# Attention scores in groups of three, maxima by head over all keys, and the maxima's split on GpSimd

## The chip, the cores and the metric

The kernel runs on one core of one Trainium2 chip. The metric is the device time of one execution in microseconds (us). The core has five engines with a queue each, and an engine works through its queue in order: PE (TensorE, matrix products; PEld is its loading of weights), DVE (VectorE), ACT (ScalarE), POOL (GpSimd) and SP (SyncE, which issues DMAs here). [...]

## The reference

Two sandwiched layers on x of 8 batches x 1024 tokens x 256 features: attention with 16 query heads of 16 features and 4 key/value heads, then a linear layer with ternary weights. All in float32.

```python
# x: (8, 1024, 256); H = 16, Hkv = 4, hd = 16
def attn(x):
    q = rope(x @ Wq); k = rope(x @ Wk); v = x @ Wv      # k, v: 4 heads, each used by 4 query heads
    scores = einsum('bhqd,bhkd->bhqk', q, k) / sqrt(256)
    o = einsum('bhqk,bhkd->bhqd', softmax(scores), v)
    return o.reshape(B, S, D) @ Wo

def ffn(x):
    delta = 0.7 * mean(abs(weight))
    w = where(weight > delta, 1, where(weight < -delta, -1, 0)) * alpha
    return einsum('bsd,od->bso', x, w) + bias

x = x + layernorm(attn(layernorm(x)))
x = x + layernorm(ffn(layernorm(x)))
```

## The kernel before

**Units, blocks, steps.** The work goes in 16 units of 512 query tokens, half a batch each. A unit has four blocks (the four query heads j of each of the four key/value heads r, so a block holds four heads x 512 queries), and a block has eight steps, one for each 128 keys: 512 steps in all. `NSTEP`, `SPU` = 32 steps in a unit, `NK` = 8 steps in a block, `UQ` = 512.

**Scores twice.** The scores are computed in two layouts. For the maximum of each query (line 569, tiles `sm`) queries are the weights of the product and 512 keys stream through, so that queries lie on the partitions; DVE then takes the maximum over the keys (line 577, into `mx`). For the exponentials (line 624, tiles `se`) 128 keys are the weights and 512 queries stream, so that keys lie on the partitions; ACT takes exp into `e` (line 632), and `e` is the streaming operand of the product with v (line 645, tile `av`). The maximum of each query is subtracted inside the second product: it rides in two more rows of the queries' operand `q_st`. These rows are made from `mx` by `shift_split` (lines 585 to 590, three small DVE operations: the larger of the two key halves, its high part, its low part), then by `shift_rows`: a transpose on PE (`pm`, line 596), a copy by ACT (`mh`, line 598) and two DMAs from SP's queue (line 605).

**Halves of the array.** Each of these score products has a contraction over 64 rows, so it takes one half `a` (0 or 1) of PE's rows, and two products on different halves can run at once. The product with v has 128 rows and 32 columns: four of them, one for each r, take the four column groups. It is in plain float32 and PE runs it as two passes, so that the profile counts two matmuls for each of the program's.

**The order.** PE, DVE and ACT get their instructions in the order in which the program writes them; POOL gets an order from the planner of the framework, but for the start and the end of the kernel, where its order is written out as well. `step(n)` (line 997) writes one step: `exp_half(n, r2)` and `max_half(k, r2)` are generators that give one score product each, interleaved as se, sm, se, sm, four of each in a step. The sm belong to a step that is `LEAD` = 11 steps ahead. A maximum tile has two banks, which hold the two halves `a` for the same 512 keys: its two products are on different halves of the array, and the reduce gives two values per query. After the scores come the parts of other work that are due in this step (`todo`), and last `av_step(n - 1)`, the four products of the step before with v over 512 queries, 128 keys.

**Other work.** `P_PARTS` and `T_PARTS` (lines 896 to 912) give the step at which each part of the projections of a later unit (`Project`) and of the tail of an earlier unit (`Tail`: output projection, layer norms, ternary layer) is written. Their products go through one bank of the pool of `se`, and are called `pq`, `pkv`, `pa`, `pf` (256 columns each, 12, 12, 12 and 8 of them in a part), `pt_xt`, `pt_ot` (four transposes in a part) and `ptv`. POOL does their elementwise work (layer norm applied, rotation of q, splits in high and low parts).

**Buffers.** In PSUM: two maximum tiles of two banks (`ps_mx`), three banks for `se` and all other products (`ps_e`), one for `av` (`ps_av`). `e` tiles: four buffers of 128 x 2 x 512.

**Ends.** In the last 11 steps the maxima are done; then `se` goes to the maximum tiles' banks, two halves in one, and one ACT instruction takes the exponential of 1024 columns (line 635).

Of the kernel before, what the change touches and what calls it, by code (L numbers as in the profile page):

```python
# [17 lines left out]
H = 16  # query heads  # L18
HKV = 4  # key/value heads, r below; query head = 4 * r + j
G = H // HKV  # L20
HD = 16
UT = 4  # token tiles in a unit
UQ = UT * P  # tokens in a unit
# [5 lines left out]
def kernel(  # L29
# [18 lines left out]
    """Two sandwiched layers: x += LN(attn(LN(x))), x += LN(ffn(LN(x))).  # L48

    The work goes in units of 512 query tokens.  Scores are computed twice: with queries on the  # L50
    partitions for each row's maximum, and with keys on the partitions for exp and the product
    with V.  For the scores q and k are split into high + low parts of 12 significant bits, which
    single-pass float32r products carry exactly: the contraction runs over
    [q_hi, q_hi, q_lo] against [k_hi, k_lo, k_hi].  The maximum, split alike, rides into the second
    pass as two more rows of the contraction, against rows of -1 in the keys.  V carries columns
    of ones, which give the softmax's denominators.  Heads r = 2 * r2 + a take the row half a of
    TensorE in the scores, and its column group r in the product with V.
    """
# [10 lines left out]
    SPU = G * NK  # steps in a unit  # L69
    NSTEP = NU * SPU  # L70
    LEAD, START = 11, 10  # steps by which the maxima run ahead, and do so at the start
# [6 lines left out]
    ep = ctx.enter_context(tc.tile_pool(name="ep", bufs=4))  # L78
# [17 lines left out]
    # ---- constants and weights  # L96
# [35 lines left out]
    # Operands with parts that never change: rows of -1 in k, of 0 in q, columns of ones in v.  # L132
# [7 lines left out]
    def fill_rows(st, value, lo, n):  # L140
        """Rows lo .. lo + n of each half."""
        flat = "p c t -> p (c t)" if len(st.shape) == 3 else "p j c t -> p (j c t)"
        for a in range(2):
            dst = st[64 * a + lo : 64 * a + lo + n].bitcast(F32).rearrange(flat)
            width = dst.shape[1]
            nc.sync.dma_start(
                out=dst, in_=fill_d[value : value + 1, 0:width].to_broadcast([n, width])
            )
# [15 lines left out]
    def split(eng, hi, lo, src, hi_eng=None):  # L164
        """src in two parts of 12 significant bits."""
        split_hi(hi_eng or eng, hi, src)
        split_lo(eng, lo, src, hi)

    # Weights in parts.  The columns of w_q go by their place in a pair.
# [9 lines left out]
    # A bank of PSUM for all that is not scores or their product with v.  Before and after those,  # L179
    # the banks of the maxima serve as well.  # L180
# [9 lines left out]
    # Ternary weights, transposed: wt[d, o] = (w[o, d] > delta) - (w[o, d] < -delta)  # L190
# [4 lines left out]
    def measure():  # L195
        ffn["ones"] = work.tile([P, P], F32, tag="qt", name="ones")
# [33 lines left out]
    # ---- layernorm over the last axis of [P, 2, D]  # L230
    def ln_stats(src):
        """(mean, -mean, 1 / sqrt(var + eps)) of each tile."""
# [29 lines left out]
    def transposed(src, tag, name, copy=nc.scalar.copy):  # L262
        """[P, 2, D] -> [P, ND, 2 * P], features on the partitions."""
# [6 lines left out]
        dst = work.tile([P, ND, 2 * P], F32R, tag=tag, name=name)  # L270
# [3 lines left out]
    TERMS = ((0, 0), (0, 1), (1, 0))  # parts of the operands in a product  # L274
# [4 lines left out]
    def product(out, left, right, terms=TERMS):  # L279
        """The sum of left[i][:, c]^T right[j][:, c]."""  # L280
# [13 lines left out]
    def rotate(eng, x, cos, sin, t2):  # L294
        """x of [P, 2, n], the two of a pair on the same partition, in place."""
# [5 lines left out]
    # ---- projections of a unit: q and k rotated, transposed and split, v.  q comes out transposed,  # L301
    # with the two columns of a pair on the same partition.
    dq = {}

    class Project:
        """Its parts, each with at most one use of PSUM.  k's pairs are rotated with tokens on the
        partitions in the first units, and in the others by a way over DRAM."""

        def __init__(self, u, eng):
# [4 lines left out]
            if u not in (1, 2):  # L314
# [3 lines left out]
                self.xs = [xs[:, :, 2 * p : 2 * p + 2, :] for p in range(2)]  # L318
            else:  # the unit before still holds those
# [4 lines left out]
                    ep.tile([P, 2, 2, D], F32R, tag="e", name=f"xs_{u}_{p}") for p in range(2)  # L324
# [9 lines left out]
        def hi(self, p, eng=None):  # L334
            split_hi(eng or self.eng, self.xs[p][:, 0], self.xn[p])

        def lo(self, p, eng=None):
            split_lo(eng or self.eng, self.xs[p][:, 1], self.xn[p], self.xs[p][:, 0])
# [7 lines left out]
        def x(self, p, l):  # L346
            self.xt[p, l] = transposed(self.xs[p][:, l], f"xt{l}", f"xt{l}_{self.u}_{p}")

        def kv(self, p):
            """k and v, transposed."""  # L350
# [8 lines left out]
        def v(self):  # L359
            """v, and k where it doesn't go over DRAM, with tokens on the partitions."""  # L360
# [33 lines left out]
        def k(self):  # L394
            """Its parts, transposed, one on each half of the partitions."""
# [7 lines left out]
            self.hl["k"] = qkp.tile([P, UQ], F32R, tag="hlk", name=f"hlk_{self.u}", bufs=2)  # L403
            nc.scalar.copy(self.hl["k"], pt.bitcast(F32))

        def kv_and_dram(self):
            """And k to [(token tile, pair), place, token]."""
# [10 lines left out]
        def kt(self):  # L418
# [3 lines left out]
            )  # fmt: skip  # L422
# [20 lines left out]
        def rotate_q(self, p, eng=None):  # L443
# [3 lines left out]
            t2 = work.tile([P, 2, 2 * P], F32, tag="t2", name=f"t2_{self.u}_{p}")  # L447
# [25 lines left out]
        def stack_keys(self):  # L473
            """[hi, hi, lo] of k in each row half."""
# [9 lines left out]
    def row_pickers():  # L484
        """Matrices that pick the rows of the stacks of q and of k, and k's rows of -1."""
# [22 lines left out]
    class PickRows:  # L508
        """Stacks of the first units, by products with those matrices."""
# [26 lines left out]
    def stack_queries(u):  # L536
        """[hi, lo, hi] of q in each row half."""
# [9 lines left out]
    # ---- each query's largest score, of the four heads of a block (unit, j)  # L547
    mx = {}

    def block_queries(i, r2=slice(None)):  # L550
        """The queries of a block in their stack: of head j, or in the last unit of a token tile."""
# [5 lines left out]
    def max_half(k, r2):  # L557
        i, m = divmod(k, NK)
        u = i // G
        ch, t = divmod(m, UT)  # L560
        queries = block_queries(i, r2)
        queries = queries[:, t * P : (t + 1) * P] if u < NU - 1 else queries[:, t]
        ks = k_st[(u // UPB) % 3]
        if m == 0 and r2 == 0:
            mx[i] = small.tile([P, 2, UT, 2, 2], F32, tag="mx", name=f"mx_{i}")
        sc = ps_mx.tile([P, 2, 512], F32, tag="sm", name=f"sm_{i}_{m}_{r2}")
        for a in (1, 0):
            rows = slice(64 * a, 64 * a + 64)
            nc.tensor.matmul(  # L569
                sc[:, a, :],  # L570
                queries[rows],
                ks[rows, r2, ch * 512 : (ch + 1) * 512],
                start=True,
                stop=True,
            )
            yield
        nc.vector.tensor_reduce(mx[i][:, ch, t, :, r2], sc, AX.X, ALU.max)  # L577

    mhl = {}

    def shift_split(i):
        """The maxima of a block, split."""
        m = mx.pop(i)
        mc = small.tile([P, UT, 2, 2], F32, tag="mc", name=f"mc_{i}")
        nc.vector.tensor_tensor(mc, m[:, 0], m[:, 1], ALU.max)
        hl = mhl[i] = small.tile([P, 2, 2, 2 * UT], F32R, tag="mhl", name=f"mhl_{i}")
        order = "(r t)" if i // G < NU - 1 else "(t r)"
        hi, lo = (hl[:, :, l].rearrange(f"p a {order} -> p t a r", r=2) for l in range(2))
# [567 lines left out]
```

## Time and profile before

| | |
|---|---|
| median of 3 runs | 1691.28 us (1685.82 to 1694.91) |
| profiled execution, its span | 1693.0 us |
| granted PE clock in the profiled execution, mean | 0.988 of full |
| maxima: DVE reduces, line 577 | 1024 x 1.217 us mean |
| exponentials: ACT, line 632 | 2004 x 0.605 us mean |
| score products on PE, lines 624 and 569 | 2048 each, 64x512 |
| products with v on PE, line 645 | 4096 passes of 128x512, 0.606 us mean, overlapped |
| POOL busy | 834.1 us (49% of the span) |

A profile row gives a line of the kernel, engine, operation, the output and input tiles, the shapes, the count, then the busy time and the mean length of one; after the second bar stands the idle time of the engine just before these instructions and what ended most of it. Matmuls overlap in PE, and their ends are modelled, so starts of PE's instructions tell more than lengths. A timeline row gives the start, the length, and what was run; neighbours of one kind are merged.

### The profile page before, as it was taken

Reading aid. Unit: us, or ns where it says so; the run is one execution under the profiler, and the core shown is the slowest. Engines: PE = TensorE matmul, PEld = TensorE weight load, DVE = VectorE, ACT = ScalarE, POOL = GpSimd, SP = SyncE. Lnnn points to the kernel's source line nnn. Section 1 sums busy time; section 2 is a strip of 40 time slices with the busy share of each in tenths; the row PEclk is TensorE's granted clock in tenths of the full one; section 3 lists DMA queues with packets and bytes.
Section 4 is the critical chain, followed back from the end, with each engine's and each line's share of the span. In section 5 each row is a group of like instructions: output and inputs, shape, how many; then the busy total and the mean of one; then the engine's idle time right before and its main releaser. Section 6 shows DMA issues by size and latency. Waiting matters only on the chain.

```text
span 1693.0 us, 27812 instructions
## 1 busy us (share of the span) xinstructions
PE 1572.8 (93%) x10200; PEld 712.9 (42%) x10200; DVE 1404.3 (83%) x1815; ACT 1254.2 (74%) x2457; POOL 834.1 (49%) x1239
## 2 busy tenths in 40 slices
PE   7989989999999999999999999999999999999998
PEld 5534343443434444443443434444443443333344
DVE  7877778888898888978888898888888888888884
ACT  4667767777777777777777777777777777777775
POOL 5543364473734637454473735637464362333354
PEclk8999999999999999999999999999999999999999
DMA  4341424134251412514133251412414132141100
GB/s 135 71 90 30 97 68 101 46 79 85 65 96 52 85 58 79 98 48 97 58 73 79 72 101 44 92 53 72 86 53 92 46 79 61 32 85 33 41 14 26
DMA packets 86040, 117.38 MB, mean 69 GB/s; under 512 B 12088, under 2 KB 50808, under 8 KB 85752
## 3 DMA queue, kind: packets, MB, share of 16 engines
q1 hardware_dynamic: 85904, 115.60, 29.7%
q8 instruction: 81, 1.33, 0.3%
q14 instruction: 55, 0.45, 0.1%
HBM read 68.65 MB, written 45.88 MB: 68 GB/s over the span
## 4 chain that ended last, share of the span: by engine, by line
PE 52%; DVE 18%; POOL 10%; ACT 10%; issue 6%; DMA 3%; SPq 1%; POOLq 0%; DVEq 0%; ACTq 0%
PE av L645 19%; PE se L624 17%; DVE mx L577 13%; ACT e L632 9%; PE sm L569 3%; PE pa L283 3%; PE pf L283 2%; PE pq L283 2%; PE pt_xt L267 2%; POOL hl L162 1%; PE pt_ot L267 1%; PE pkv L283 1%; DVE bnst L237 1%; DVE mhl L589 1%; POOL t L297 1%
## 5 line engine op out<-in xcount | busy, mean ns | idle before, releaser
L577 DVE TENSOR_REDUCE mx<-sm 128x2 f32<-128x1024 f32 x1024 | 1199.6, 1217 | 246.2 <-PE se L624 176.4
L632 ACT ACTIVATE e<-se 128x512 f32<-128x512 f32 x2004 | 1045.7, 605 | 315.0 <-PE sm L569 286.8
L624 PE MATMUL se<-q_st,k_st 64*128 64x512 f32 x2048 | 739.4, 445 | 77.7 <-ACT e L632 53.6
L569 PE MATMUL sm<-k_st,q_st 64*128 64x512 f32 x2048 | 758.3, 460 | 12.0 <-DVE mx L577 10.8
L624 PEld LDWEIGHTS se<-q_st,k_st 64*128 64x128 f32 x2048 | 338.5, 185 | 699.1 <-ACT e L632 432.6
L645 PE MATMUL av<-e,v_aug 128*32 128x512 f32 x4096 | 548.1, 606 | 0.0
L569 PEld LDWEIGHTS sm<-k_st,q_st 64*128 64x128 f32 x2048 | 327.2, 185 | 59.1 <-DVE mx L577 42.5
L241 POOL TENSOR_SCALAR lnsc<-mv 128x2 f32<-128x2 f32 (+1 forms) x134 | 26.1, 194 | 432.6 <-DVE mv L239 427.6
L645 PEld LDWEIGHTS av<-e,v_aug 128*32 128x32 f32 x4096 | 80.8, 108 | 87.7 <-issue 53.6
L780 POOL TENSOR_TENSOR a<-a,bias_bc 128x512 f32<-128x512 f32 x30 | 38.4, 1280 | 144.7 <-ACT a L779 144.7
L719 POOL TENSOR_TENSOR xn<-xn,a 128x512 f32<-128x512 f32 x30 | 38.4, 1280 | 122.7 <-DMA a<-d_rec 114.4
L242 POOL TENSOR_TENSOR lnsc<-lnsc,mhalf 128x2 f32<-128x2 f32 (+1 forms) x134 | 92.2, 688 | 0.9
L162 POOL TENSOR_TENSOR hl<-xn,hl 128x512 fp32r<-128x512 f32 x60 | 76.4, 1284 | 0.5
L253 POOL TENSOR_SCALAR xn<-x,lnsc 128x256 f32<-128x256 f32 x116 | 64.8, 566 | 3.5
L283 PE MATMUL pa<-woh,hl 128*128 128x256 f32 x240 | 47.3, 296 | 2.6 <-POOL hl L162 1.2
L237 DVE BATCH_NORM_STATS2 bnst<-a 128x6 f32<-128x256 f32 x120 | 44.5, 413 | 4.1 <-POOL a L780 4.1
L297 POOL TENSOR_TENSOR t<-q_rot,sin_q_sb 128x512 f32<-128x512 f32 x31 | 39.7, 1280 | 14.5 <-ACT q_rot L438 14.3
L283 PE MATMUL pq<-xt,wqkvh 128*128 128x256 f32 x256 | 45.9, 303 | 0.2 <-ACT e L632 0.2
L237 DVE BATCH_NORM_STATS2 bnst<-x 128x6 f32<-128x256 f32 x124 | 46.0, 413 | 0.2 <-DMA x<-in_L_attn_x 0.2
L271 ACT CAST xt<-pt_xt 128x512 fp32r<-128x512 f32 x64 | 39.1, 617 | 4.4 <-PE pt_xt L267 4.4
L271 ACT CAST ot<-pt_ot 128x512 fp32r<-128x512 f32 x66 | 40.7, 618 | 1.9 <-PE pt_ot L267 1.9
L162 POOL TENSOR_TENSOR hlq<-q_rot,hlq 128x512 fp32r<-128x512 f32 x31 | 39.7, 1282 | 4.7 <-ACT hlq L159 4.5
(155 smaller groups left out, 1273.9 us busy)
## 6 DMA issues: line engine op xcount, KB each, us to landing
q_st<-dq SPq DMA_DIRECT2D x90, 256.0 KB
dq<-hlq SPq DMA_DIRECT2D x60, 256.0 KB
d_av<-avsb SPq DMA_DIRECT2D x60, 256.0 KB
x<-in_L_attn_x SPq DMA_DIRECT2D x15, 512.0 KB
xn<-d_av SPq DMA_DIRECT2D x30, 256.0 KB
a<-d_rec SPq DMA_DIRECT2D x30, 256.0 KB
xr<-in_L_attn_x SPq DMA_DIRECT2D x15, 512.0 KB
out_x<-a SPq DMA_DIRECT2D x30, 256.0 KB
```

The source lines that it names most:

```text
L162: eng.tensor_tensor(lo, src, hi.bitcast(F32), ALU.subtract)
L237: nc.vector.bn_stats(st[:, t, :], src[:, t, :])
L242: nc.gpsimd.tensor_tensor(sc[:, 1, :], sc[:, 1, :], mhalf[:, :n], ALU.pow)
L253: eng.tensor_scalar(dst[:, t, :], src[:, t, :], sc[:, 0, t : t + 1] if eng is nc.gpsimd else mv[:, t, 0:1], sc[:, 1, t : t + 1], ALU.add i ...
L271: copy(dst, pt.bitcast(F32))
L283: nc.tensor.matmul(out, chunk(left[i], c), chunk(right[j], c), start=(k == 0), stop=(k == len(steps) - 1),)
L297: eng.tensor_tensor(dst, x, table.unsqueeze(1).to_broadcast(list(x.shape)), ALU.mult)
L569: nc.tensor.matmul(sc[:, a, :], queries[rows], ks[rows, r2, ch * 512 : (ch + 1) * 512], start=True, stop=True,)
L577: nc.vector.tensor_reduce(mx[i][:, ch, t, :, r2], sc, AX.X, ALU.max)
L624: nc.tensor.matmul(sc if len(queries.shape) == 2 else sc.rearrange("p (j t) -> p j t", j=G), ks[rows, r2, kt * P : (kt + 1) * P], queries[ ...
L632: nc.scalar.activation(e[:, a, :], sc, AF.Exp, scale=1.0 / D**0.5)
L645: nc.tensor.matmul(av_ps[0][32 * r : 32 * r + 32, :], va[:, kt, r, :], e[r // 2][:, r % 2, :], start=(kt == 0), stop=(kt == NK - 1),)
```

## The change

The order of the work is written by groups instead of steps. A *quarter* is one score product of the exponential kind, four to a step; a block has 32 quarters.

- A group ("window") has three quarters: three se and three sm, alternating, then the parts of other work of any step that ended in this group, then the product with v for the group that lies two groups back. Of a block's 32 quarters, ten groups take three and the last two. One group at the start has two so that the maxima's order comes out; the last 11 steps go in groups of four.
- The product with v of a group takes as many columns as the group has quarters, times 128: the columns of all eight steps of a block are counted through, 4096 in all, and a group of three takes 384 of them. Where these cross from one step's 512 to the next's, two pieces are issued, each for all four r (`av_piece`). It accumulates into the same `av` bank.
- A maximum tile has the same size as before, but holds both halves of the keys for one `a`, that is one head: its two sm are on the same half of the array, and the reduce gives one value per query. (In the first block the order before is kept.) The larger of two key halves is no longer taken by an operation of its own.
- The split of the maxima in a high and a low part goes from DVE to POOL.
- `e` tiles hold 512 columns; there are 12 of them. The half `a` changes every two quarters instead of every quarter. Some small buffers become single or move, to make room.
- In the last 11 steps each 512 columns of exponentials are an ACT instruction of their own.

The comments and docstrings of the kernel are gone in the changed version, which does nothing to the program.

```diff
-    ep = ctx.enter_context(tc.tile_pool(name="ep", bufs=4))
+    ep = ctx.enter_context(tc.tile_pool(name="ep", bufs=12))
...
-    def max_half(k, r2):
...
+    def max_scores(v):
+        i, k = divmod(v // 2, 2 * NK)
+        u, part = i // G, v % 2
+        if i == 0:
+            a, ch, t, r2 = 1 - part, k // NK, k // 2 % UT, k % 2
+        else:
+            a, ch, t, r2 = 1 - k % 2, part, k // 4, k // 2 % 2
...
+        nc.tensor.matmul(
+            sm[0][:, part, :],
+            queries[rows],
+            k_st[(u // UPB) % 3][rows, r2, ch * 512 : (ch + 1) * 512],
...
+        else:
+            nc.vector.tensor_reduce(mx[i][:, a, t, r2 : r2 + 1], sm[0], AX.XY, ALU.max)
+        if k == 2 * NK - 1:
+            shift_split(i)
+            due.append((v // 4 + (1 if i < 2 else 2), i))
...
     def shift_split(i):
         m = mx.pop(i)
-        mc = small.tile([P, UT, 2, 2], F32, tag="mc", name=f"mc_{i}")
-        nc.vector.tensor_tensor(mc, m[:, 0], m[:, 1], ALU.max)
...
-        nc.vector.tensor_copy(hi, mc)
-        nc.vector.tensor_tensor(lo, mc, hi.bitcast(F32), ALU.subtract)
+        split(nc.gpsimd, hi, lo, m)
...
+    def exp_one(s):
+        n, (a, r2) = s // 4, divmod(s % 4, 2)
+        i, kt = divmod(n, NK)
+        e = es[n, r2, a] = ep.tile([P, UQ], F32, tag="e", name=f"e_{i}_{kt}_{r2}_{a}")
+        sc = ps_e.tile([P, 512], F32, tag="se", name=f"se_{i}_{kt}_{r2}_{a}")
+        exp_scores(n, r2, a, sc)
+        nc.scalar.activation(e, sc, AF.Exp, scale=1.0 / D**0.5)
...
+    def av_piece(i, first, end):
...
+        for kt in range(first // UQ, (end - 1) // UQ + 1):
+            lo, hi = max(first - kt * UQ, 0), min(end - kt * UQ, UQ)
+            for r in (1, 2, 3, 0):
+                nc.tensor.matmul(
+                    av_ps[0][32 * r : 32 * r + 32, lo:hi],
+                    va[:, kt, r, :],
+                    es[i * NK + kt, r // 2, r % 2][:, lo:hi],
+                    start=(kt == 0 and lo == 0),
+                    stop=(kt == NK - 1 and hi == UQ),
+                )
...
+    def maxima_by(s):
+        return s + 4 * START + 2 * (s >= 28) + 2 * (s >= 36)
...
+    def parts_of_step(n):
+        if due and due[0][0] <= maxima_by(4 * n + 4) // 4 - 1:
+            shift_rows(due.pop(0)[1])
+        for f, args in todo.pop(n, ()):
+            f(*args)
...
+    def window(i, s, size, late):
+        if done:
+            av_out(done.pop())
+        if late:
+            for r2 in range(2):
+                exp_two(s // 4, r2)
+        else:
+            end = min(maxima_by(s + size), 4 * NSTEP)
+            for q in range(max(size, end - maxima[0])):
+                if q < size:
+                    exp_one(s + q)
+                if maxima[0] < end:
+                    max_scores(maxima[0])
+                    maxima[0] += 1
+        behind.append((i, s, size))
+        for n in range(s // 4, (s + size) // 4):
+            parts_of_step(n)
+        av_windows(1 if late else 2)
```

## The prediction

> **What bounds the kernel now.** I read the page's busy shares and costliest groups first, then single steps on the timelines of PE, DVE and ACT, then the interval between units.
>
> ```profile
> span 1693.0 us, 27812 instructions
> ...
> PE 1572.8 (93%) x10200; PEld 712.9 (42%) x10200; DVE 1404.3 (83%) x1815; ACT 1254.2 (74%) x2457; POOL 834.1 (49%) x1239
> ...
> L577 DVE TENSOR_REDUCE mx<-sm 128x2 f32<-128x1024 f32 x1024 | 1199.6, 1217 | 246.2 <-PE se L624 176.4
> L632 ACT ACTIVATE e<-se 128x512 f32<-128x512 f32 x2004 | 1045.7, 605 | 315.0 <-PE sm L569 286.8
> ```
>
> PE is never long idle, and DVE's and ACT's idle time ends with scores from PE. But 93% is not 93% of work; one step shows that. Columns: start, length, instructions.
>
> ```profile
> 811.63 0.50 PE L624 MATMUL se<-q_st,k_st 64*128 64x512 f32 x1
> ...
> 812.81 0.50 PE L624 MATMUL se<-q_st,k_st 64*128 64x512 f32 x1
> ...
> 813.25 1.07 PE L645 MATMUL av<-e,v_aug 128*32 128x512 f32 x8
> 814.24 0.49 PE L624 MATMUL se<-q_st,k_st 64*128 64x512 f32 x1
> ...
> 814.58 0.62 PE L624 MATMUL se<-q_st,k_st 64*128 64x512 f32 x2
> 814.85 0.49 PE L569 MATMUL sm<-k_st,q_st 64*128 64x512 f32 x1
> 815.42 0.49 PE L624 MATMUL se<-q_st,k_st 64*128 64x512 f32 x1
> ...
> 816.00 0.50 PE L267 MATMUL pt_xt<-ident_r,xs 128*128 128x128 f32 x4
> 816.43 1.06 PE L645 MATMUL av<-e,v_aug 128*32 128x512 f32 x8
> ```
>
> ```profile
> 812.44 2.35 DVE L577 TENSOR_REDUCE mx<-sm 128x2 f32<-128x1024 f32 x2 [0.30 <-PE se L624]
> 815.04 2.36 DVE L577 TENSOR_REDUCE mx<-sm 128x2 f32<-128x1024 f32 x2 [0.25 <-PE se L624]
> ```
>
> ```profile
> 814.77 2.06 ACT L632 ACTIVATE e<-se 128x512 f32<-128x512 f32 x4 [0.55 <-PE sm L569]
> ```
>
> I call one se and the sm issued with it a pair. A step without other work lasts 814.24 - 811.63 = 2.61 us: pairs at 0, 0.34, 0.6 and 1.18, the v product 0.44 after the last (812.81 to 813.25), and 0.99 more to the next step. The fourth pair comes late because there are three banks for se: ACT starts 0.53 after the first se, takes 0.60, and the bank is free at 815.37. That wait (0.35 us) is what groups of three remove. DVE's reduce starts 0.46 after a tile's second sm; two follow 1.14 apart (2.35 - 1.21), so DVE waits only 0.25 to 0.30 of 2.61.
>
> ```profile
> L706 DVE RECIPROCAL den<-den x10: 540/542/544, 402.3 to 1312.3; 128x64 f32<-128x64 f32 x10
> ```
>
> This runs once a unit, so a unit takes 910.0 / 9 = 101.1 us. Its 32 steps clean are 83.5; 17.6 come from the other work. From last-pair-to-v-product intervals less 0.44, that is on PE: five of 12 matmuls (pq, pa, pkv) 1.67 each, two pf 1.19, eight groups of transposes 0.57 (815.42 to 816.43), ptv 0.43, four pm 0.21: 16.6. The last 1.0 is DVE and ACT.
>
> **The change, part by part.**
>
> *Groups of three.* A block (32 quarters; eight steps before) becomes ten groups of three pairs and one of two. An unblocked group has pairs at 0, 0.34, 0.6, then 0.35 to 0.44, then the v product. The two rounds of that start about 0.46 apart (1.07 less the row's mean of 0.605); a quarter fewer columns takes 0.115 off each: 0.99 - 0.23 = 0.76, bounds 0.74 (all scales) and 0.99 (nothing does). I take 0.77. That makes 1.75 a group, 3.5 for six quarters against 3.92 now: a gain, if nothing else waited.
>
> *The tiles that straddle.* Something else does. Three pairs are one and a half maximum tiles, and there are still two tiles. Call the tiles of two groups A, B, C: B gets its first half in the third pair of one group and its second in the first pair of the next, after the v product. From that pair: 0.56 to B's reduce (0.46, and the first matmul after a v product lasts 0.50 where later ones last 0.39), 1.14 to C's, 1.21 for it, 0.05 to the sm that was waiting for C's buffer (a reduce that ended at 804.66 released the one at 804.71). That sm is the next B's first half, in a third pair; behind it in PE's queue are the v product and the next group. So 0.44 + 0.77 more, and the cycle closes: 0.56 + 1.14 + 1.21 + 0.05 + 0.44 + 0.77 = 4.17 us for six quarters, 0.25 more than now, with PE standing 0.6 in every second group. A block: 5 x 4.17, and the short group 0.34 + 0.44 + 0.77 = 1.55, less some 0.4 that its whole tile and its 256 columns give back: 22.0 against 20.9. A unit: +4.5. The three se banks no longer bind: a bank is free 1.18 after its se and is wanted after 1.75.
>
> *What hides in the wait.* Groups of odd place (they end with C whole) have 0.6 us of room; in the others each microsecond goes straight into the cycle. By the due steps, modulo 8, parts at 0, 2, 3, 5, 6 fall into odd groups: six transposes (3.4), ptv (0.4), one pq and one pf (0.6 each can hide): 5.0 a unit. All of it stood on the path before. Ends: nothing, and 20 x 0.6 = 12.
>
> *Split v products.* Every fourth 512 columns end inside a group, so five of the eleven are issued as 128 and 256 columns: two more rounds of four matmuls. Nothing in the trace is so narrow in column groups; a round's four weight loads (0.108 us each, partly together) may outlast 128 columns. From 0.05 for both rounds to 0.7 (each as long as a full one); nearest are the transposes of 128 columns, four in 0.34 (0.50 less 0.16), little over their streaming, so 0.15. Three a block lie where nothing hides them: 3 x 4 x 0.15 = +1.8.
>
> [...]
>
> *Split of the maxima to GpSimd.* DVE loses L585, L589 and L590, about 0.62 a block; DVE has spare time except in the 2.35 of B and C, so a quarter counts: -0.6 a unit (0 to -2.5). POOL is in order. In the block whose maxima end while q is rotated it is full:
>
> ```profile
> 850.45 1.28 POOL L297 TENSOR_TENSOR q_rot<-q_rot,cos_q_sb 128x512 f32<-128x512 f32 x1
> 851.70 0.70 POOL L242 TENSOR_TENSOR lnsc<-lnsc,mhalf 128x2 f32<-128x2 f32 x1
> 852.37 0.72 POOL L298 TENSOR_TENSOR q_rot<-q_rot,t 128x256 f32<-128x256 f32 x1
> 853.06 0.72 POOL L299 TENSOR_TENSOR q_rot<-q_rot,t 128x256 f32<-128x256 f32 x1
> 853.78 1.08 POOL L253 TENSOR_SCALAR xn<-x,lnsc 128x256 f32<-128x256 f32 x2
> ```
>
> In the changed order the high part stands before L298 and the low part after L253: done near 855.4 with two small operations of 0.2 to 0.35 each, where PE's transpose pm ran at 853.15. PE is in order, so the v product and all scores stand behind it. The distance from pq to pm grows from 8.3 to about 8.8 us, so 1.7 of wait, 0.6 of it in an odd group's room: +1.0 a unit (0 to 2.4). In the other three blocks POOL is idle before pm or has 3 us to spare: nothing.
>
> *pm to the first se of its block.* The two DMAs of the maxima were issued 1.06 to 2.4 us after pm (802.35, 803.40, 1.35 for both) and had landed by 806.37, where the se ran without a wait: 2.4 to 4.0 after pm. Now only two v products and the short group lie between, 2.6. Up to 1.4, I take 0.7; three of a unit's four short groups carry a pq, pa or pf that covers it: +0.7 a unit (0 to 5.6). SP issues the same DMAs in the same order.
>
> The rest is worth nothing: the twelve smaller e tiles are released two groups ahead of use; the last eleven steps give ACT four exps of 0.49 instead of two of 1.03.
>
> Sum: 4.5 - 5.0 + 1.8 - 0.6 + 1.0 + 0.7 = +2.4 us a unit; over 15 units (the pipeline's start and the late steps left out, taken as unchanged within 5) +36 on the span of 1693.0, 1729. The median of the runs is 1.7 below that execution: 1727.
>
> **Rivals.** *The removed wait wins (faster).* For it: 0.35 us of waiting leave each step, PE and DVE shares are 93% and 83%, and PE with no wait would need 4 x (10 x 1.75 + 1.55 + 0.75) + 16.6 = 96 a unit. It needs more than 7.4 us of the other work under DVE's wait instead of 5.0, for instance because parts in even groups delay the reduces less than PE. At 97.5 a unit: 1693 - 54 - 2 = 1637. Against: the cycle through B and C holds whatever PE does. *Nothing hides:* parts and statistics on DVE fall between B and C, so that the 5.0 is lost: +7.4, 1802. *Narrow rounds cost full:* 0.7 instead of 0.15: +6.6 a unit more, 1826. *GpSimd late in every block:* 1.7 in four blocks: +5.8 more, 1814; POOL's idle time before pm in three blocks speaks against it.
>
> **How the numbers follow.** Forecast (slower by 0.5 to 4.5%) 0.42; nothing hides, narrow rounds or a late GpSimd 0.23 together; the wait's removal wins 0.27; cases that cancel within 0.5%, about what three runs (0.27% around their median) can tell, 0.08. Slower 0.65, same 0.08, faster 0.27. The likeliest's own range is 1700 to 1770; the range takes in half of each side: 1637, the faster rival's price, and 1814, that of the late GpSimd.
>
> **What would show it.** The changed trace should have pairs of groups near 1.7 and 2.5 us, with third pairs released by DVE mx; L632's waits on PE fewer and no se waiting for ACT e; a unit near 103.5; one pm a unit waiting for POOL. Wrong it is if groups of 1.7 follow each other without that wait, if reduces stand end to end, or if v products of two pieces last over 1.1.

## The result, and the profile after

| | before | after |
|---|---|---|
| median | 1691.74 us | 1828.04 us (1826.63 to 1832.48, 4 runs) |
| ratio to before, 95% interval | | 1.0813 [1.0793, 1.0832] |
| span of the profiled execution | 1693.0 us | 1830.4 us |
| mean granted PE clock | 0.988 | 0.951 |
| first reciprocal of a unit | 192.2 us | 212.2 us |
| first to last of 15 reciprocals | 1397.9 us | 1511.4 us |
| from the last one to the end | 102.9 us | 106.8 us |

The kernel became 8.1% slower; 1727 was forecast, with a range from 1637 to 1814. The three lower rows add up to the difference of the spans: 20.0 at the start, 113.5 in the units, 3.9 at the end. (Of the four runs of `e2` below one was in a slow state, 1935.27 us at a clock of 0.643, and is left out of its median.) Of the page of the changed kernel, these lines answer to those shown of before (the PEclk line is the granted clock in 40 slices, in tenths):

```profile
span 1830.4 us, 35785 instructions
...
PE 1628.5 (89%) x14208; PEld 853.9 (47%) x14208; DVE 1366.8 (75%) x1624; ACT 1270.5 (69%) x2479; POOL 861.3 (47%) x1367
...
PEclk8989899998999989999998999999999999999998
...
L590 DVE TENSOR_REDUCE mx<-sm 128x1 f32<-128x1024 f32 x1008 | 1194.0, 1220 | 418.3 <-PE sm L576 351.9
L642 ACT ACTIVATE e<-se 128x512 f32<-128x512 f32 x2004 | 1057.5, 602 | 383.9 <-PE sm L576 320.5
L627 PE MATMUL se<-q_st,k_st 64*128 64x512 f32 x2048 | 711.5, 446 | 81.9 <-DMA q_st<-mh 80.4
```

Reduces and exps last what they lasted (1.22 and 0.60 us). DVE and ACT idle more, mostly for scores from PE, and PE is busy 89% instead of 93%. Something holds PE itself, and the last line names it: the maxima's rows on their way into the queries' stack.

The rows of the reciprocal give the unit: 884.2 / 8 = 110.5 us in this stretch, where before had 101.1. (Over all 14 intervals the difference is 113.5 / 14 = 8.1 us, a little less.)

```profile
L723 DVE RECIPROCAL den<-den x9: 541/543/544, 440.6 to 1324.8; 128x64 f32<-128x64 f32 x9
```

PE's waits in that stretch of eight units (total us, times, longest):

```profile
PE se L627 <- DMA q_st<-mh: 43.3, 17, 3.5
PE pm L609 <- POOL mhl L162: 18.5, 8, 3.6
PE sm L576 <- DVE mx L590: 8.0, 47, 0.2
PE pt_xt L267 <- ACT e L642: 6.6, 27, 0.3
```

Before, the first of PE's waits was se for ACT's e, 33.2 us in 153 pieces over nine units; se no longer waits for it, as the change meant. But the products of other work, which take a bank from the same pool, now wait for ACT's e in small pieces (pt_xt, pt_ot, pm, pa, pf and pq: 18.3 us, 2.3 a unit), where the same view of before lists none. In place of se's wait stand three long waits a unit: twice the first se of a block (5.4 us together), once pm (2.3).

The pm first. POOL's timeline, then PE's, in the block where q is rotated:

```profile
823.48 0.71 POOL L242 TENSOR_TENSOR lnsc<-lnsc,mhalf 128x2 f32<-128x2 f32 x1
824.16 0.22 POOL L157 TENSOR_SCALAR mhl<-mx 128x16 fp32r<-128x16 f32 x1
824.32 0.74 POOL L298 TENSOR_TENSOR q_rot<-q_rot,t 128x256 f32<-128x256 f32 x1
825.02 0.72 POOL L299 TENSOR_TENSOR q_rot<-q_rot,t 128x256 f32<-128x256 f32 x1
825.73 1.09 POOL L253 TENSOR_SCALAR xn<-x,lnsc 128x256 f32<-128x256 f32 x2
826.79 0.23 POOL L162 TENSOR_TENSOR mhl<-mx,mhl 128x16 fp32r<-128x16 f32 x1
```

```profile
827.07 0.24 PE L609 MATMUL pm<-ident_r,mhl 128*32 128x128 f32 x1 [2.12 <-POOL mhl L162]
827.24 0.92 PE L662 MATMUL av<-e,v_aug 128*32 128x384 f32 x8
828.09 0.79 PE L627 MATMUL se<-q_st,k_st 64*128 64x512 f32 x1
...
829.24 1.22 PE L283 MATMUL pq<-xt,wqkvh 128*128 128x256 f32 x4
```

The low part of the split stands in POOL's queue behind 2.5 us of the rotation and a norm. And the stand has an echo: the se after it lasts 0.79 instead of 0.50, four matmuls of pq 1.22 instead of 0.73. The granted clock was 0.50 from 827.9 to 831.3.

Then the first se of a unit, on SP (DMA issues) and PE:

```profile
853.34 0.78 SPq L542 DMA_DIRECT2D q_st<-dq  x2
854.60 1.37 SPq L618 DMA_DIRECT2D q_st<-mh  x2
```

```profile
853.62 0.22 PE L609 MATMUL pm<-ident_r,mhl 128*32 128x128 f32 x1 [0.15 <-ACT e L642]
...
856.36 0.85 PE L662 MATMUL av<-e,v_aug 128*32 128x384 f32 x8
860.35 0.46 PE L627 MATMUL se<-q_st,k_st 64*128 64x512 f32 x1 [3.14 <-DMA q_st<-mh]
```

The rows arrive 6.7 us after pm, 5.75 after their issue. Two transfers of 256 KB for the next unit's queries were issued just ahead of the two of 8 KB. Before, at the same place of a unit, the order was the other one:

```profile
881.00 1.36 SPq L605 DMA_DIRECT2D q_st<-mh  x2
882.47 4.45 SPq L541 DMA_DIRECT2D q_st<-dq  x6
```

The windows from the issue of the rows to the first se tell the difference by the DMA share: 1.07 in the changed kernel, and 0.41 before, in a block of the same kind. (Their columns: stretch, length, busy us of PE, PEld, DVE, ACT and POOL with counts, clock, DMA share, GB/s.) In the changed kernel the rows share busy DMA engines with what was started ahead of them:

```profile
854.60:860.35 5.75, 2.62 (x24) 1.45 (x21) 2.77 (x6) 1.77 (x3) 2.79 (x5) 1.00 1.07 141
```

```profile
779.80:783.90 4.10, 3.88 (x30) 1.97 (x26) 3.69 (x6) 2.75 (x5) 0.11 (x1) 1.00 0.41 81
```

The next block, the other one whose first se waits, has a load of 512 KB issued half a microsecond ahead of the rows; before, it was issued behind them (804.87, the rows at 803.40):

```profile
882.12 0.39 SPq L91 DMA_DIRECT2D x<-in_L_attn_x  x1
882.60 1.37 SPq L618 DMA_DIRECT2D q_st<-mh  x2
```

What the split of work itself does can be read where no such wait is near:

```profile
811.23 0.86 PE L662 MATMUL av<-e,v_aug 128*32 128x128 f32 x16
812.02 0.50 PE L627 MATMUL se<-q_st,k_st 64*128 64x512 f32 x1
...
813.31 0.50 PE L576 MATMUL sm<-k_st,q_st 64*128 64x512 f32 x1 [0.17 <-DVE mx L590]
813.74 0.86 PE L662 MATMUL av<-e,v_aug 128*32 128x256 f32 x16
814.52 0.50 PE L627 MATMUL se<-q_st,k_st 64*128 64x512 f32 x1
```

A group whose third sm waits for DVE lasts 814.52 - 812.02 = 2.50, as forecast. One that does not wait, and has its v product in one piece:

```profile
818.11 0.50 PE L627 MATMUL se<-q_st,k_st 64*128 64x512 f32 x1
...
819.00 0.85 PE L662 MATMUL av<-e,v_aug 128*32 128x384 f32 x8
819.78 0.50 PE L627 MATMUL se<-q_st,k_st 64*128 64x512 f32 x1
```

It lasts 1.67. The v product in two pieces takes 0.79 (811.23 to 812.02), that in one piece 0.78 (819.00 to 819.78); over all groups at full clock whose next se did not wait, the medians are 0.788 (288 groups) and 0.783 (269). The two rounds more cost next to nothing.

### The profile page after: what moved, and what is told of

Same layout as the page of the kernel before. It is cut to its first block, busy times and chain, and to the rows that moved or that the text cites. A ratio compares the mean times of both kernels' runs of the same rounds, so it can differ in the third digit from the quotient of the medians.

```text
span 1830.4 us, 35785 instructions
## 1 busy us (share of the span) xinstructions
PE 1628.5 (89%) x14208; PEld 853.9 (47%) x14208; DVE 1366.8 (75%) x1624; ACT 1270.5 (69%) x2479; POOL 861.3 (47%) x1367
## 4 chain that ended last, share of the span: by engine, by line
PE 50%; DVE 15%; DMA 13%; ACT 9%; POOL 8%; issue 4%; SPq 1%; POOLq 0%; DVEq 0%
PE av L662 19%; PE se L627 15%; DVE mx L590 13%; ACT e L642 7%; DMA q_st<-mh 7%; PE sm L576 5%; PE pa L283 3%; PE pq L283 2%; DMA d_k<-kv_t 2%; PE pt_xt L267 2%; DMA k_rot<-d_k 1%; PE pt_ot L267 1%; POOL xn L253 1%; PE pkv L283 1%; PE pf L283 1%
## 5 line engine op out<-in xcount | busy, mean ns | idle before, releaser
L590 DVE TENSOR_REDUCE mx<-sm 128x1 f32<-128x1024 f32 x1008 | 1194.0, 1220 | 418.3 <-PE sm L576 351.9
L642 ACT ACTIVATE e<-se 128x512 f32<-128x512 f32 x2004 | 1057.5, 602 | 383.9 <-PE sm L576 320.5
L627 PE MATMUL se<-q_st,k_st 64*128 64x512 f32 x2048 | 711.5, 446 | 81.9 <-DMA q_st<-mh 80.4
L576 PE MATMUL sm<-k_st,q_st 64*128 64x512 f32 x2048 | 746.0, 459 | 21.6 <-DVE mx L590 19.6
L662 PE MATMUL av<-e,v_aug 128*32 128x256 f32 (+2 forms) x8104 | 611.9, 403 | 0.0
L576 PEld LDWEIGHTS sm<-k_st,q_st 64*128 64x128 f32 x2048 | 335.9, 192 | 110.8 <-DVE mx L590 84.0
L662 PEld LDWEIGHTS av<-e,v_aug 128*32 128x32 f32 x8104 | 188.8, 111 | 188.0 <-issue 136.4
L157 POOL TENSOR_SCALAR mhl<-mx 128x16 fp32r<-128x16 f32 x64 | 13.9, 217 | 160.9 <-DVE mx L590 160.9
L797 POOL TENSOR_TENSOR a<-a,bias_bc 128x512 f32<-128x512 f32 x30 | 38.6, 1285 | 102.8 <-ACT a L796 102.5
L609 PE MATMUL pm<-ident_r,mhl 128*32 128x128 f32 x64 | 14.7, 230 | 47.0 <-POOL mhl L162 38.9
L283 PEld LDWEIGHTS pq<-xt,wqkvh 128*128 128x128 f32 x256 | 40.9, 221 | 16.0 <-ACT e L642 8.5
```

The costliest lines, as they stand in the source:

```text
L283: nc.tensor.matmul(out, chunk(left[i], c), chunk(right[j], c), start=(k == 0), stop=(k == len(steps) - 1),)
L576: nc.tensor.matmul(sm[0][:, part, :], queries[rows], k_st[(u // UPB) % 3][rows, r2, ch * 512 : (ch + 1) * 512], start=True, stop=True,)
L590: nc.vector.tensor_reduce(mx[i][:, a, t, r2 : r2 + 1], sm[0], AX.XY, ALU.max)
L627: nc.tensor.matmul(sc if len(queries.shape) == 2 else sc.rearrange("p (j t) -> p j t", j=G), k_st[(i // G // UPB) % 3][rows, r2, kt * P : ...
L642: nc.scalar.activation(e, sc, AF.Exp, scale=1.0 / D**0.5)
L662: nc.tensor.matmul(av_ps[0][32 * r : 32 * r + 32, lo:hi], va[:, kt, r, :], es[i * NK + kt, r // 2, r % 2][:, lo:hi], start=(kt == 0 and lo ...
```

## The experiments

My theory after the result: the attention loop is about as fast as before, and the loss lies on the maxima's way from DVE to the first se (split, pm, DMA), with the halved clock behind each stand. Rivals: the straddling tiles, or GpSimd alone.

**The split alone back on DVE** (`e1`).

```
-        split(nc.gpsimd, hi, lo, m)
+        nc.vector.tensor_copy(hi, m)
+        nc.vector.tensor_tensor(lo, m, hi.bitcast(F32), ALU.subtract)
```

> The changed kernel with the maxima's split back on DVE (two small operations), nothing else. Theory A (the loss is PE standing at the maxima's path: pm behind POOL, then the first se of a block behind the DMA of the maxima's rows, and PE's clock halved after each such stand): the 39 us of pm waiting for POOL go, and with them a third of the half-clock stretches; about 1775 us, clock 0.96 to 0.97 instead of 0.951, no pm waiting for POOL. Theory B (the loss is the cycle through the straddling maximum tiles, which lengthens every second group): nothing of that changes; 1820 to 1835 us.

1809.72 us, ratio 1.0676 [1.0644, 1.0709], unit 108.3: a miss, far from the 1775 of the first theory. pm no longer waits, but se's waits for the rows grow from 80.4 to 92.5. GpSimd is a part of the loss, not most of it.

**And pm one step earlier** (`e2`).

```
-            due.append((v // 4 + (1 if i < 2 else 2), i))
+            due.append((v // 4 + 1, i))
```

> As the kernel with the split on DVE, and the transpose pm of each block written one step earlier, so that the copy and the two DMAs of the maxima's rows start some 3 us earlier. Theory A: the 80 us in which se waits for these rows fall under 20 and the clock returns to about 0.985; 1665 to 1700 us. Theory B: as with the split on DVE alone.

1710.69 us (median of three runs), ratio 1.0091 [1.0065, 1.0116], 99 less than `e1` and 11 above the range of its theory. Unit and waits over nine units:

```profile
L724 DVE RECIPROCAL den<-den x10: 541/542/543, 409.1 to 1317.9; 128x64 f32<-128x64 f32 x10
```

```profile
PE se L628 <- DMA q_st<-mh: 9.4, 10, 1.3
PE sm L576 <- DVE mx L590: 9.1, 54, 0.2
```

The unit is 908.8 / 9 = 101.0, that of before, with the straddling tiles and all v products in pieces still in it. The granted clock over these units is 1.00; over the eight of the changed kernel it was 0.95. The loss was the rows' way.

**What the halved clock costs** (`e7`). Products into an unused tile are put where PE stands, so that work is added (`keep_busy(i, n)` issues n products of 512 columns into a tile that nothing reads):

```
+        if local == 27 and i % G == 2 and 8 <= i < NU * G - 12:
+            keep_busy(i, 7)
         for n in range(s // 4, (s + size) // 4):
             parts_of_step(n)
         av_windows(1 if late else 2)
+        if local == 30 and i % G in (3, 0) and 8 <= i < NU * G - 12:
+            keep_busy(i, 9 if i % G == 3 else 7)
```

> The changed kernel with idle products written into PE's queue where it stands waiting (seven before pm in the third block of a unit, nine and seven before the first se of the first and second block; about 0.21 us each, of no use to any result). They add work but no wait. If the half clock that follows a stand is part of the loss: the clock rises from 0.951 to 0.975 or more, and the time falls to 1780 to 1815 us. If only the waits cost: 1825 to 1840, whatever the clock.

1803.04 us, ratio 1.0656 [1.0638, 1.0674], clock 0.981 instead of 0.951: 253 useless products of 0.40 us, and 25 us less. (The records of neighbours overlap: at full clock, products of this form started 0.23 us apart in the kernel before, sixteen in 3.88 us, where the expectation counted 0.21.) They stand in 11 of the 16 units; where they do, the unit falls by 3.0, from 110.5 to (1292.6 - 432.6) / 8 = 107.5:

```profile
L723 DVE RECIPROCAL den<-den x9: 543/543/544, 432.6 to 1292.6; 128x64 f32<-128x64 f32 x9
```

A second estimate, from `e2`: a unit of the changed kernel without its two kinds of stand is 110.5 - 5.4 - 2.3 = 102.8, that of `e2` without its own (9.4 / 9) 100.0; the clock's share is about 2.8 a unit, some 40 in all.

**The split on GpSimd in the kernel before** (`e5`): the same edit as `e1`, backwards, with mc.

> The kernel before with one part of the change alone: the high and the low part of the maxima made by POOL instead of DVE. Theory A (GpSimd's place in the chain is part of the loss): pm waits for POOL in one block of each unit; from 1 to 3 us a unit with the half clock behind it, 1710 to 1740 us. If the old order's longer way from pm to se hides it: 1690 to 1700.

1746.90 us, ratio 1.0323 [1.0302, 1.0344], 53 us more than before on the same chip (1693.95) and more than expected. One stand a unit is enough:

```profile
PE pm L595 <- POOL mhl L162: 36.1, 15, 3.1
```

These are 36 of the 53 us, and the clock fell from 0.988 to 0.971: the expectation named the half clock, but priced it too low.

**pm early, split on GpSimd** (`e11`): the edit of `e2` to due alone.

> The changed kernel with pm one step earlier and nothing else; the split stays on GpSimd. In the changed kernel the split is done 2.5 to 2.9, 5.1 and 6.5 us before pm in three blocks of a unit and PE waits 1.9 to 2.6 for it in the last. pm moves by some 3 to 4 us. Theory (the rows' path from pm to se is the larger loss, the split the smaller): the waits of se for DMA fall from 80 to below 35; pm waits 4.5 to 6 for GpSimd in the last block and below 1.5 in the first; one or two stands a unit in place of three, 1735 to 1780. Rival (GpSimd is the larger loss): pm waits over 2 in two or more blocks and the time is above 1800.

1852.89 us, ratio 1.0945 [1.0909, 1.0981], the rival's side. The rows then come in time (7.9 instead of 80.4), but pm is moved towards the maxima, into the time that GpSimd needs:

```profile
PE pm L609 <- POOL mhl L162: 135.5, 29, 9.9
...
PE se L627 <- DMA q_st<-mh: 7.9, 2, 7.4
```

So most of the gain needs both the early pm and the split on DVE (the split alone -18, pm alone +25, both -117). Either GpSimd is late whatever the distance, or the whole way from the last maximum to the first se is too short.

**The maxima a step further ahead** (`e12`): the way gets longer, pm and split keep their place on it in steps.

```
-        return s + 4 * START + 2 * (s >= 28) + 2 * (s >= 36)
+        return s + 4 * START + 2 * (s >= 28) + 2 * (s >= 36) + 4 * (s >= 200)
```

> The changed kernel with its maxima one step (four quarters) further ahead of the exps from the second unit on; pm keeps its distance from the maxima, and the split stays on GpSimd. pm then stands two groups earlier before the first se that needs its rows. Theory (what is missing is time between the last maximum of a block and its first se; moving pm alone towards the maxima took it from GpSimd instead): se waits for DMA below 25 in all where the changed kernel has 80, the wait of pm for GpSimd stays at 25 to 45, one stand a unit in place of three; as far as the split on DVE gained by the early pm (98 us), less the stand that is left: 1725 to 1765. Rival (GpSimd is late whatever the distance, as with pm early: 135 us of waits of pm): pm waits above 60 and the time above 1790.

1749.74 us, ratio 1.0335 [1.0292, 1.0377], as the theory expected: 78 us less with the split on GpSimd.

```profile
PE pm L609 <- POOL mhl L162: 37.8, 15, 6.0
PE se L627 <- DMA q_st<-mh: 22.6, 11, 8.1
```

The trace shows where the way had become short. From the last reduce of a block's maxima to its first se, stands taken off, the kernel before has 9.7, 7.7, 11.4 and 9.6 us in the four blocks of a unit (medians), and the changed one 8.7, 8.2, 11.1 and 8.8: at most 0.9 less. The part behind pm lost more: from pm to the first se, at full clock, before has 5.0, 4.0, 5.4 and 5.5, the changed one 3.6, 2.5, 4.0 and 4.0. `e12` has 10.2 to 14.2 for the whole way, and at least 6.6 behind pm.

**The maxima's DMAs from ACT's queue** (`e3`): `nc.scalar.dma_start` for `nc.sync.dma_start` in line 618.

> The changed kernel with the two DMAs of the maxima's rows issued from ACT's queue instead of SP's, where two 256 KB loads and a 512 KB load stand just ahead of them in two of a unit's four blocks. If SP's order is what makes the rows late: the waits of se for them fall from 80 us to under 40, and 1760 to 1790 us. If the rows are late because the time from pm to se is too short whatever stands ahead, or because the transfers share the DMA engines: within 10 us of 1828. Theory B: 1820 to 1835.

1886.64 us, ratio 1.1137 [1.1117, 1.1157]: a miss. se waits 117.1 for the rows, in the first block of a unit 5.0 to 5.8 instead of 3.1 to 3.5, although they were issued 1.0 us after pm as before. SP had meanwhile issued all six 256 KB transfers, begun 1.3 us ahead of the rows, and from their issue to the first se (7.6 us) the DMA share is again 1.07:

```profile
876.20:883.80 7.60, 2.62 (x24) 1.43 (x21) 2.77 (x6) 1.66 (x3) 4.49 (x7) 1.00 1.07 131
```

So it is not the queue of the issue that delays the rows in this block, but the transfers that run when they start.

**Whole tiles in a group** (`e4`): four sm and two in turn, so that no tile straddles.

```
-            end = min(maxima_by(s + size), 4 * NSTEP)
+            end = min((maxima_by(s + size) + 1) // 2 * 2, 4 * NSTEP)
```

> The changed kernel with groups of three exponentials and, in turn, four and two maximum products, so that no maximum tile straddles a product with v. Theory B: the pair of groups goes from 4.2 to about 3.8 us, 20 pairs a unit: 1720 to 1770 us. Theory A: the shorter groups are taken up by longer waits for the maxima's rows and for POOL; 1800 to 1830 us, with more than 119 us of those waits.

1830.81 us, ratio 1.0804 [1.0786, 1.0822]: nothing, although sm's wait for DVE fell from 19.6 to 2.3. The straddling tiles are not what bounds the changed kernel; its units wait at the rows' way. Groups without other work did get shorter, as meant: 1.93 and 1.68 us (medians at full clock) in place of 2.51 and 1.68.

**Whole tiles, split on DVE, pm early** (`e6`), and the same with the second unit's queries stacked three steps later at the start (`e8`).

> Split on DVE, pm one step earlier, and whole maximum tiles (four and two maximum products in turn). With the waits at the maxima's path mostly gone, the pair of groups can now fall from 4.17 to about 3.4 us, DVE's own pace: up to 20 x 0.77 = 15 us a unit, of which some 5 were hidden by other work before and some will turn into waits of se for the maxima's rows again. 1570 to 1650 us. If the straddling tiles cost nothing: 1705 to 1715, as without whole tiles.

> As whole tiles with pm early, and the six 256 KB loads of the second unit's queries written three steps later, so that the maxima's rows of the second block stand ahead of them in SP's queue. The 14 us stand of PE near 92 to 106 us should fall under 8: 5 to 10 us less than without.

1697.85 us, ratio 1.0020 [1.0002, 1.0037], and 1695.45, ratio 1.0028 [1.0008, 1.0048]. The first is far from its 1570 to 1650. It is 13 us under `e2`, but not by its units: the mean of all 14 intervals is (1597.3 - 203.3) / 14 = 99.6 us in `e6`, 99.1 in `e8` and 99.3 in `e2`. What takes back the 0.6 us that whole tiles give to a pair of groups stays open. The second's stand at the start (14.6 us at 102.5) did not go.

**Block 3's maxima from ACT in `e8`.** In `e9` the condition was `i == 3`, in `e10` `i % G == 3`.

> As the kernel with whole tiles, the early pm and the later stack (1695.45), and the two transfers of block 3's maxima alone are issued from ACT. There PE stood 14.6 us at 102.5, since SP issued the maxima 10.5 us after the copy of mh, behind two groups of other transfers; the rows then landed 8 us later. From ACT they are issued within 1 us of the copy. Theory (SP's order makes the start late): the stand falls below 5, the first reciprocal comes 9 to 12 us earlier, 1684 to 1688. Rival (the rows are late because of the transfers that run at the time, not because of the place in the queue): the stand stays above 10 and the time within 3 of 1695.

> The same for the last block of every unit, which in that kernel has PE wait 1.0 to 1.9 us a unit while SP issues six transfers of k ahead of the maxima (7.2 to 7.7 us after pm instead of 1.07). Theory (a transfer's place in the queue sets these waits too): they go, 1.2 x 14 = 17 less two issues on ACT a unit (the kernel with all maxima from ACT lost 58 us for 128 issues, 0.45 each: 13 for 30), so 5 less to 3 more than the kernel with ACT for block 3 alone. Rival (ACT's time is free there): 13 to 18 less than it.

`e9`: 1697.04 us, ratio 1.0038 [1.0017, 1.0058]. The stand is that of block 1, which the edit did not touch, so it tells nothing of it. `e10`: 1756.87 us, ratio 1.0383 [1.0356, 1.0410], a miss: ACT stood at its issue (4.2 us idle before the copy of v_aug at 680.51), and se then waited up to 5.3 us for v_aug, queued behind it on ACT.

**The step further ahead with split on DVE and whole tiles** (`e13`), and **all of it with the early pm, the late stack and block 1's first maxima from ACT** (`e14`).

> The same with the split on DVE and whole maximum tiles in each group; pm at its distance of two steps. Theory: no stand over 1.5 us is left after the pipeline's start, the granted clock stays full there, se waits for DMA below 25 of which some 15 at the start; the unit is at most 100.0 (the kernel with whole tiles and the early pm had 100.9, of which about 1.3 was the wait before block 3): 1670 to 1693. Rival (the wait before block 3 was hiding ACT and DVE, and goes into other waits): 1694 to 1702.

> Whole tiles, split on DVE, pm a step early, the later stack, and the maxima a step further ahead; the maxima of block 1 of the first unit alone are sent from ACT (the run that meant to remove the 14.6 us stand before that block took block 3 and left it). Theory: the stand at about 100 us falls below 6, the first reciprocal comes by 195 instead of 200 to 203, and the waits before block 3 go: 1665 to 1685, faster than before by 0.4 to 1.5%. Rival (the rows are late through the transfers that run beside them; ACT waits there and delays the exps): the stand stays above 10: 1685 to 1700.

`e13`: 1718.10 us, ratio 1.0143 [1.0115, 1.0171], a miss; its unit is 101.1 and its first reciprocal comes at 211.2. `e14`: 1688.20 us, ratio 0.9965 [0.9946, 0.9984], the only version with all its work that is faster than before, by 0.35%. The waits for rows are gone from its units, which last 898.9 / 9 = 99.9:

```profile
L725 DVE RECIPROCAL den<-den x10: 543/543/545, 405.1 to 1304.0; 128x64 f32<-128x64 f32 x10
```

The start stayed: the issue on ACT came at 94.31, 8.7 us after the copy of mh had ended, and PE stood 8.3 us (behind a copy of q that ACT had queued after that issue) and 2.5 us. What that issue waits for the trace doesn't tell; it is not SP's queue, which it no longer stands in.

**Half of each reduce left out** (`e15`, `e14` with `sm[0][:, 1:]` reduced).

> As the kernel with whole tiles, the split on DVE, the early pm and the maxima a step ahead (1688.20, unit 99.9), but each maximum is taken over the second half of its tile's columns alone; the first half is left out, so a reduce has 512 columns instead of 1024. In that kernel DVE is busy 85.2 us of a unit, 78 of them reduces, and PE waits for no row of the maxima; ACT is busy 78.1. Theory (without stands DVE's reduces set the rows' pace, and what PE does beside attention starves them, so that a clean pair of groups of 3.4 us counts for little): the unit falls by 5 or more, to 90 to 95, the time to 1530 to 1630. Rival (PE's own issue, with 44 v products a unit where 32 were, is the limit): the unit stays above 98 and the time above 1660.

1631.51 us, ratio 0.9623 [0.9602, 0.9644], unit (1268.4 - 490.4) / 8 = 97.2: between both theories.

```profile
L644 ACT ACTIVATE e<-se 128x512 f32<-128x512 f32 x2004 | 1058.0, 603 | 223.4 <-PE se L629 128.4 <-PE sm L576 81.5
L590 DVE TENSOR_REDUCE mx<-sm 128x1 f32<-128x512 f32 x1008 | 671.1, 688 | 688.6 <-PE sm L576 618.8 <-PE se L629 68.6
```

Half of DVE's reduces (1183.7 - 671.1 over 15.75 units, 32.5 us a unit) are worth 2.7 of 99.9, and DVE then idles for PE. The limit that is left is mostly PE's issue. By starts (each of PE's instructions priced from its start to the next one's), its unit in `e14` is 33.8 of v products, 51.2 of scores and 14.9 of other work; before it was 31.9, 54.3 and 15.0. Scores gain 3.1, and the v products give 1.9 back: 40 of 0.78 and 4 of 0.57 instead of 32 of 0.99.

## Why the prediction was wrong

The direction was right (slower), and the amount was not: +2.4 us a unit forecast, +9.4 measured, and 20 us at the start where 5 were allowed.

- *Groups of three, straddling tiles.* The mechanism was right. Groups of 1.7 and 2.5 us in turn were forecast, 4.17 for a pair; where groups without other work follow each other at full clock, the trace has 1.68 and 2.51 in turn, 4.19. The wait moved to the third sm, as described. But such a run begins with two or three short groups: of 175 pairs of neighbouring groups 43 are both under 2.3 us, which the prediction had called a sign of being wrong, and which makes the tiles' term less than its 4.5. And "The three se banks no longer bind" holds for se alone: other work's products wait 2.3 a unit for a bank.
- *What hides in the wait, split v products, DVE's relief.* The sum of these with the tiles was 4.5 - 5.0 + 1.8 - 0.6 = +0.7. `e2`, where the other terms are nearly gone, has a unit of 101.0, or 100.0 without its stand: -1.1. (Its split is on DVE, so that most of the relief of 0.6 isn't in it.) The split v products were priced at 0.15 for two rounds and cost 0.01; that is 1.7 of the difference; no run tells the tiles' 4.5 from the hidden 5.0. The faster rival (97.5 a unit) failed: even `e14`, without straddling tiles or stands, has 99.9.
- *GpSimd late at one pm a unit.* The mechanism, the place and the order in POOL's queue were right. The size was not: 1.0 net (0 to 2.4), measured 2.3 of stand, and the clock behind it. In `e5` the same edit alone cost 53 us: 3.9 a unit (105.0 instead of 101.1, with a stand of 2.8 in it), and 9.6 at the start.
- *pm to the first se: the step that failed.* It said "Up to 1.4, I take 0.7", and "SP issues the same DMAs in the same order". The stands were 5.4 a unit. The distance was right (2.5 measured, and 3.6 in the block with pf). Two things were wrong. I took the landing time of one quiet block (2.4 to 4.0 after pm) for all; here the rows came 6.5 to 7.1 after pm in block 0 and 4.5 to 4.8 in block 1. And SP's order did not stay: two 256 KB transfers of the next unit came ahead of the maxima in block 0, and a 512 KB load in block 1; `e3` shows for block 0 that what is started ahead is what delays them. The upper bound that I wrote down, 5.6, held the stand; I chose from the lower end, counting on pq, pa and pf as cover. They covered two blocks; pf in block 0 did not.
- *The halved clock: no term at all.* Every sum in the prediction priced a stand at its length. The clock's share is 25 us at least (`e7`, in 11 units), some 40 by the second estimate: about 3 a unit by both.
- *The start, "taken as unchanged within 5".* It lost 20.0: pm waited 8.7 us for GpSimd at 91.3, where the split stood behind a rotation of k that itself had waited for its DMA until 87.0, and se 7.8 for the rows at 106.3, where before waits 4.6 for them at 91.9. Only with the split on GpSimd does pm wait there (`e5` reached its first reciprocal at 201.8), but `e2`, without it, came to 207.8, with 14.3 us of se's wait. What holds the rows there stays open.

With the measured sizes the unit adds up: -1.1 for the attention loop, +5.4 and +2.3 for the stands, +2.8 for the clock, +9.4 in all (the clock's term is the remainder by its definition; what supports it is `e7`, with 3.0).

## What to carry to other kernels

When a loop is re-cut, look first at the longest chain of small steps that crosses engines and queues (here reduce, split, transpose, copy, DMA, first score): its slack per block counts, in each kind of block, and cutting a wait elsewhere can use it up. Moving a step to a less busy engine (`e5`: 53 us more), or closer to its source (`e11`: 25 more), can spend the same slack; moving the source ahead adds to it (`e12`: 78 less). Here a stand of PE of more than 2 us mostly cost more than its length: half clock followed 18 of the 21 in eight units.

## What the runs showed of the hardware

In the units of the changed kernel half clock came in stretches of 3.4 or 6.8 us (at its start also 10.2 and 13.7). In eight of these units 88.7 of 884 us were granted at 0.50, and of 24 stands of PE over 1.5 us, all 12 above 2.4 us had such a stretch begin in them or within 1.8 us of their end, as had 6 of 9 between 2.0 and 2.4, and none of 3 below. Two rows of granted clock (stretch, length, then busy us of PE, PEld, DVE, ACT and POOL, clock, DMA share, GB/s) show the 3.4 us right after the stand at 827.07, and a stretch after that at full clock:

```profile
827.90:831.30 3.40, 3.40 (x17) 2.57 (x14) 1.92 (x5) 1.09 (x2) 2.76 (x3) 0.50 0.03 10
835.00:850.00 15.00, 14.09 (x131) 7.58 (x132) 12.71 (x15) 13.06 (x26) 12.34 (x18) 1.00 0.27 88
```

PE is busy for the whole 3.40 us of the first, at half clock. Of the 18 stands that half clock followed, 16 lasted 2.1 to 3.4 us, no longer than the shortest of its stretches. Why 3 of the 9 stands between 2.0 and 2.4 us had none behind them, no run shows.

A v product's matmuls of 128 columns in four column groups added next to no time in the changed kernel: 384 columns took 0.788 us in two pieces and 0.783 in one (medians at full clock).
